# A two-layer cross-attention kernel: the order in the first attention, and a new list of pieces in the second

## The chip, the cores and the metric

The kernel runs on one NeuronCore of a Trainium2 chip. The metric is the device time of one execution in microseconds. A core has five engines that work side by side, each with its own queue in program order: PE (matrix products and transposes, results into PSUM), DVE (vector work), ACT (activations and copies), POOL [...] and SP (which here only issues transfers). They wait for each other through semaphores. [...]

## The reference

All data is float32. `x` and `ctx` have shape (32, 256, 256): batches, tokens, features. The program has two layers.

```python
# L0: 16 heads of 16 features; only batch 0 of the attention is used
q, k, v = heads(x @ Wq.T), heads(ctx @ Wk.T), heads(ctx @ Wv.T)
att = softmax(q @ k.T / 4) @ v
x1 = x + att[0]                       # att of batch 0 is added to every batch

# L1
nX = layernorm(ctx, n1w, n1b)
nF = layernorm(x1, n2w, n2b)
attended = softmax(nF @ nX.T / 16) @ nX          # first attention of L1
h = gelu(attended @ fc1_w.T + fc1_b)             # 4 hidden values
cross = h @ fc2_w.T + fc2_b
nC = layernorm(cross, n3w, n3b)
self_att = softmax(nC @ nC.T / 16) @ nC          # second attention of L1
out = nF + gamma2 * (cross + gamma1 * self_att)
```

Since `cross` is linear in 4 hidden values and a constant, the second attention is done in rows of 5 or 6 values per token rather than 256. Its products have a contraction of at most 32.

## The kernel before

Everything is one function, with a manual schedule: instructions stand on each engine in the order in which the Python code issues them. No scheduler moves them, so a line moved in the code is a line moved in the queues of all the engines that it uses. Batches are handled in fours (`QB = 4`; eight fours, `NQ = 8`).

**L0** (line 680 on). The 16 heads of batch 0 are handled as four fours, `j` = 0 to 3. For each four:
- `head_queries(j)`: the scores by queries, 8 matmuls on PE into four PSUM banks (`four_banks`, which goes round six banks);
- `head_maxima(j, sq, heads)`: DVE takes the row maxima, one instruction of 128 x 512 for each of the four banks;
- `head_less(j)`: PE transposes the maxima (`pm`), and the function that it returns lets DVE add them to the queries (`qmT`);
- `head_keys(j)`: the scores by keys with the maxima in them, then four exponentials on ACT;
- `head_values(j)`: the weighted values and sums on PE (`ph`), and a copy of the column block, `col`, by ACT or DVE;
- `head_turned(j)`: PE transposes the block, and the function that it returns (`weighted`) lets DVE divide and write `att`.

Between these stand `project_values`, the second half of the value projection; `stats(n)`, DVE's statistics of the context of batch n (two instructions of 0.41 us each); `moments_c(q)`, eight short POOL instructions for the layer norm of a four of contexts; `even_normed` (POOL) and `odd_normed` (ACT), which apply it to the even and odd token tile; and `setup_bias`, a small product with DVE's `fc1b_all` behind it, which the first hidden layer needs much later. When `att` is complete, it is added to batch 0 by DVE and to fours of batches by an accumulating DMA that POOL issues (`add_attention`).

Short results of PE go to PSUM tiles of the tag `tp`, of which there are two. A new one takes the bank that was freed first.

**First attention of L1** (`first_step(s)`, one step for each batch, and three more to drain). `scaled_at` says in which step POOL multiplies the skip of batch n by its norm weight (`scale_skip(n)`, one POOL instruction of 128 x 512). Parts of the second attention for early groups are put between these steps.

**Second attention of L1** (`order`, line 1244 on). After the last step the rest is written as a list of pieces, worked off word by word. Groups `g` are fours of batches, pairs `p` two batches. The words: `q7@s1+q6@et` scores by queries of pairs 7 and 6 into the banks `s1` and `et` (an even and an odd pair together use different rows of PE); `max7` DVE's maxima of them; `turn_t`, `turn_u`, `turn_v` transposes and `tT`, `uT`, `vT` the copies of them (ACT, or DVE with `.v`); `k5@s0` scores by keys, `exp5` their exponentials; `sums1` the weighted sums of a group, `col1` their copy, `turn_a1` and `a1` transpose and division; `o1@et` the output product, `add1` DVE's add to the skip and the write of two batches to memory; `scale12` the scaling of a skip. For the last eight batches the hidden layer also stands in the list: `turn_n7`, `n7`, `pre6` (POOL), `gelu6` (ACT), `m3` (POOL, product with a Gram matrix), `vg3` (DVE), `vgv3` (POOL), `var3` (DVE), `r3` (POOL: the power -1/2 and the next Gram product `w_k`), `t_k3` (DVE).

`add p` needs `scale` of both of its batches. A bank (`s0`, `s1` or the two of `et`) is free for the next product once the `max`, `exp` or `add` before has read it. `turn_u6` and `turn_u7` need `t_k3`.

Of the kernel before, what the change touches and what calls it, by code (L numbers as in the profile page):

```python
# [22 lines left out]
QB = 4  # L23
# [4 lines left out]
def tile_xattn_seq(  # L28
# [51 lines left out]
    def bank(tag, name):  # L80
        return ps.tile([P, NC, D], F32, tag=tag, name=name)
# [50 lines left out]
    k6 = const.tile([NK, D], F32)  # L132
# [80 lines left out]
    def moments(st, n, name, eng=None):  # L213

        eng = eng or nc.gpsimd

        def t(what, c=1, bufs=2):
            return small.tile([P, n, c], F32, tag=f"{what}{n}", name=f"{what}_{name}", bufs=bufs)

        sm, df, sq, v4, ve, nm = t("sm", 2), t("df"), t("sq"), t("v4"), t("ve"), t("nmean")  # L220
        rs, nmr = t("rs", 1, 3), t("nmr", 1, 3)
        eng.tensor_sub(df, st[:, :, 1:2], st[:, :, 4:5])
        eng.tensor_add(sm, st[:, :, 1:3], st[:, :, 4:6])
        eng.tensor_mul(sq, df, df)
        eng.tensor_scalar(v4, sm[:, :, 1:2], 4.0 / D, 4 * EPS, ALU.mult, ALU.add)
        eng.tensor_add(ve, v4, sq)
        nc.gpsimd.tensor_tensor(  # L227
            rs.rearrange("p n o -> p (n o)"),
            ve.rearrange("p n o -> p (n o)"),
            neg_half[:, 0:n],  # L230
            ALU.pow,
        )

        def product():
            eng.tensor_scalar(nm, sm[:, :, 0:1], -0.5, 0.0, ALU.mult, ALU.add)
            eng.tensor_mul(nmr, nm, rs)  # L236

        if eng is nc.gpsimd:
            product()
            return rs, nmr  # L240
        return rs, nmr, product
# [19 lines left out]
    def flat(st):  # L261
        return st.rearrange("p b t c -> p (b t) c")

    def moments_c(q):
        rn = moments(flat(st_of[q - 1][:, 0]), TQ, f"c{q}")
        for b in range(QB):
            mc_of[q * QB + b] = *rn, b * NC
# [159 lines left out]
    def project_values(t, copy):  # L427
        pp = bank("tp", f"pp_v{t}")
        for dc in range(NC):
            nc.tensor.matmul(  # L430
                pp[:, t, :],
                c0T[:, dc, t * P : (t + 1) * P],
                wvT[:, dc, :],
                start=(dc == 0),
                stop=(dc == NC - 1),
            )
        copy(v1[:, t, :, 0:DK], pp[:, t, :].rearrange("p (h e) -> p h e", e=DK))

    def pair_products(*pairs):

        for t in range(NC):
            for p, lhs, rhs, dst in pairs:
                for i in range(2):
                    r = SL * (p % 2 * 2 + i)
                    nc.tensor.matmul(  # L445
                        dst[i][:, t, :],
                        lhs[r : r + SL, t * P : (t + 1) * P],
                        rhs[r : r + SL, :],
                        start=True,
                        stop=True,  # L450
                    )
# [4 lines left out]
    def four_banks(name):  # L456

        at = head_banks[0]
        head_banks[0] = (at + QB) % 6
        return [  # L460
            ps0.tile([P, NC, D], F32, tag=f"h{i}", name=f"{name}_{i}")
            if i < QB
            else bank("et", f"{name}_{i}")
            for i in ((at + n) % 6 for n in range(QB))
        ]
# [8 lines left out]
    def head_of(j, i):  # L474
        return 8 * (j // 2) + 2 * i + j % 2

    def head_queries(j):

        sq = four_banks(f"sq{j}")
        qk = qT[:, j, :], kT[:, j, :]  # L480
        pair_products((0, *qk, sq[0:2]), (1, *qk, sq[2:4]))
        return sq

    def head_maxima(j, sq, heads):
        for i in heads:
            nc.vector.tensor_reduce(
                m_all[:, j % 2, :, i, ones_at[j % 2]], sq[i], AX.X, ALU.max, negate=True
            )

    def head_less(j):  # L490
        pm = bank("tp", f"pm_{j}")
        for t in range(NC):
            nc.tensor.transpose(
                pm[:, 0, t * P : (t + 1) * P],
                m_all[:, j % 2, t].rearrange("p b c -> p (b c)"),
                ident,
            )
        return lambda: nc.vector.tensor_add(qmT[:, j % 2, :], pm[:, 0, :], qT[:, j, :])

    def head_keys(j):  # L500

        sk = four_banks(f"sk{j}")
        kq = kT[:, j, :], qmT[:, j % 2, :]
        pair_products((0, *kq, sk[0:2]), (1, *kq, sk[2:4]))
        eT_of[j] = wk.tile([P, QB, NC, D], F32, tag="eTq", name=f"eT_h{j}", bufs=2)
        for i in range(QB):
            nc.scalar.activation(eT_of[j][:, i], sk[i], AF.Exp)
# [4 lines left out]
    def head_values(j, copy=nc.scalar.copy, by_pairs=False):  # L512
        col_of[j] = by_columns(
            tp_bank,
            f"h{j}",
            lambda kt, i: v1[:, kt, head_of(j, i), :],
            eT_of.pop(j),
            copy,
            by_pairs,
        )  # L520

    def head_turned(j):
        pa = tokens_first(tp_bank, col_of.pop(j), f"h{j}")

        def weighted():
            rd = small.tile([P, NC, QB, 1], F32, tag="rdh", name=f"rd_h{j}")
            nc.vector.reciprocal(rd, pa[:, :, :, DK : DK + 1])
            nc.vector.tensor_mul(
                att.rearrange("p t (k i e d) -> p t k i e d", i=QB, e=2, d=DK)[
                    :, :, j // 2, :, j % 2, :  # L530
                ],
                pa[:, :, :, 0:DK],
                rd.to_broadcast([P, NC, QB, DK]),
            )

        return weighted
# [39 lines left out]
    def setup_bias():  # L576
        pb = bank("tp", "p_b1f")
        for dc in range(NC):
            nc.tensor.matmul(
                pb[:, 0, 0:FH], ones, b1f[:, dc, :], start=(dc == 0), stop=(dc == NC - 1)  # L580
            )
        nc.vector.tensor_add(fc1b_all, pb[:, 0, 0:FH], fc1b_bc)
# [78 lines left out]
    on_scalar = nc.scalar.copy  # L661

    by_vector = nc.vector.tensor_copy

    def stats(*ns):
        for n in ns:
            stats_c(n)
# [6 lines left out]
    sq = head_queries(0)  # L674
# [5 lines left out]
    sq = head_queries(1)  # L680
# [9 lines left out]
    head_less(1)()  # L690
    setup_outer()
    stats(3)
    project_values(1, on_scalar)
    moments_c(0)
    even_normed(0, 1, 2, 3)
    sq = head_queries(2)
    stats(4)
    head_maxima(2, sq, (0, 1))
    head_values(0)
    setup_bias()  # L700
    head_maxima(2, sq, (2, 3))
    head_keys(1)
    odd_normed(0, 1)
    weighted = head_turned(0)
    stats(5)
    head_less(2)()
    weighted()
    sq = head_queries(3)
    stats(6)
    head_maxima(3, sq, range(QB))  # L710
    head_values(1)
    odd_normed(2, 3)
    head_keys(2)
    weighted = head_turned(1)
    stats(7)
    moments_c(1)
    even_normed(4, 5)
    head_less(3)()
    weighted()
    head_keys(3)  # L720
    stats(8, 9, 10)
    head_values(2, by_vector)
    stats(11)
    odd_normed(4)
    head_values(3, on_scalar, True)
    c_ends = moments_ahead(2)
    weighted = head_turned(2), head_turned(3)
    for f in weighted:
# [133 lines left out]
    ]  # L862


    scaled_at = [25, 26, 26, 27, 27, 28, 29, 29, 31, 31, 32, 32]

    first_ends = [ends]

# [373 lines left out]


    order = """
    turn_v0 scale12 q7@s1+q6@et t_k2 vT0 scale13 turn_t2 max7 sums1 tT2 scale14 max6
    k5@s0+k4@s1 col1 turn_n7 exp5 scale15 turn_u5 n7 o1@et uT5.v exp4 pre6 turn_t3 add1
    scale16 q11@s1+o0@s0 tT3 gelu6 sums2 max11 scale17 turn_u4 col2 add0 m3 turn_a1 uT4
    k7@s1+q10@et scale18 a1 vg3 turn_a2 q8@s0 max10 exp7 vgv3 scale19 turn_v1 var3
    q9@s1+k6@et a2 vT1 max8 r3 turn_v2 exp6 turn_t5 max9 o2@s0 tT5 vT2 o3@et+k10@s1 add2
    turn_t4 exp10 add3 sums3 k11@s1+o4@s0 tT4.v col3 scale20 t_k3 turn_a3 exp11 add4  # L1250
    turn_u6 scale21 o5@et uT6 a3 scale22 q12@s0+k9@s1 add5 turn_v3 exp9 scale23 max12
    sums5 k8@s1+q13@et col5.v scale24 vT3.v turn_u7 exp8 max13 scale25 o7@s0 uT7 turn_t6
    scale26 add7 q15@et+o6@s1 tT6 turn_a5 scale27 max15 sums4 a5 scale28 q14@s0+k13@et
    col4 add6 turn_a4 exp13 scale29 turn_v5 max14 k12@s1 vT5 a4 scale30 o11@s0+o10@et
    exp12 turn_t7 add11 scale31 sums6 tT7 add10 k15@s1+k14@s0 col6.v turn_v4 exp15
    turn_a6 vT4.v a6 exp14 o8@et+o9@s1 sums7 add9 turn_v6 col7 add8 vT6 turn_a7
    o13@s1+o12@s0 a7 turn_v7 add13 vT7 o14@et add12 o15@s1 add14 add15
    """

    def turn_a(g):  # L1260
# [100 lines left out]
```

## Time and profile before

| | us |
|---|---|
| three runs | 229.31, 230.23, 233.49 (median 230.23) |
| profiled execution | 233.63 |
| its span, first to last instruction | 231.9 |
| PE busy | 214.7 (93%) |
| POOL busy | 174.8 (75%) |
| DVE busy | 169.8 (73%) |
| ACT busy | 146.8 (63%) |
| mean granted PE clock | 0.969 |

The page gives busy time by engine, then the span in 40 slices of 5.8 us (a digit is a share in tenths; PEclk is the granted clock of PE), then the chain of work that ended last, and groups of instructions. A line of the timeline reads: start, duration, engine, line, operation, output<-input, shape, count, and in brackets the idle time before it with what ended it. PEld is the weight load of PE. A busy PE includes the modelled ends of pipelined matmuls.

### The profile page before, as it was taken

Reading aid. Unit: us, or ns where it says so; the run is one execution under the profiler, and the core shown is the slowest. Engines: PE = TensorE matmul, PEld = TensorE weight load, DVE = VectorE, ACT = ScalarE, POOL = GpSimd, SP = SyncE. Lnnn points to the kernel's source line nnn. Section 1 sums busy time; section 2 is a strip of 40 time slices with the busy share of each in tenths; the row PEclk is TensorE's granted clock in tenths of the full one; section 3 lists DMA queues with packets and bytes.
Section 4 is the critical chain, followed back from the end, with each engine's and each line's share of the span. In section 5 each row is a group of like instructions: output and inputs, shape, how many; then the busy total and the mean of one; then the engine's idle time right before and its main releaser. Section 6 shows DMA issues by size and latency. Waiting matters only on the chain.

```text
span 231.9 us, 4950 instructions
## 1 busy us (share of the span) xinstructions
PE 214.7 (93%) x1797; PEld 155.8 (67%) x1797; DVE 169.8 (73%) x409; ACT 146.8 (63%) x299; POOL 174.8 (75%) x276
## 2 busy tenths in 40 slices
PE   7999898898999989999999999989989999999960
PEld 6766556576787768697897887866665666566540
DVE  1797989899988748667686686766384866588791
ACT  2544978698988285966789967456846753444410
POOL 6057598576989999999979999995189999993000
PEclk9999999999999999999999999999999995699996
DMA  6789997999959964180720000000000130444477
GB/s 212 271 310 371 394 383 148 194 256 236 207 104 335 275 117 170 34 151 2 133 51 1 3 0 0 3 4 4 4 0 3 51 133 0 181 184 181 185 281 264
DMA packets 18038, 33.81 MB, mean 146 GB/s; under 512 B 1175, under 2 KB 2142, under 8 KB 18014
## 3 DMA queue, kind: packets, MB, share of 16 engines
q1 hardware_dynamic: 12974, 24.33, 29.3%
q0 software_dynamic: 3696, 7.34, 18.1%
q10 hardware_dynamic: 1344, 1.84, 2.3%
q8 instruction: 14, 0.23, 0.4%
q14 instruction: 10, 0.08, 0.1%
HBM read 17.73 MB, written 8.39 MB: 113 GB/s over the span
## 4 chain that ended last, share of the span: by engine, by line
PE 53%; POOL 23%; DVE 14%; ACT 5%; issue 2%; DVEq 0%; POOLq 0%; ACTq 0%
PE sc L779 13%; POOL x_all L770 5%; PE k L445 4%; PE pt_x L202 4%; PE o L445 3%; PE pt_c L202 3%; POOL cq L307 3%; DVE st L211 3%; PE pt_e L202 3%; PE pu L357 3%; POOL rs_b L227 3%; PE sc L445 2%; POOL rs_x L227 2%; PE ph L357 2%; PE pf L357 2%
## 5 line engine op out<-in xcount | busy, mean ns | idle before, releaser
L779 PE MATMUL sc<-nxT,nfT 128*128 128x256 f32 x256 | 62.4, 386 | 0.7 <-ACT nfT L761 0.7
L779 PEld LDWEIGHTS sc<-nxT,nfT 128*128 128x128 f32 x256 | 45.7, 190 | 12.1 <-issue 5.3
L770 POOL TENSOR_TENSOR x_all<-x_all,w_bc 128x512 f32<-128x512 f32 x32 | 39.8, 1273 | 0.0
L792 ACT ACTIVATE e<-sc,nm 128x256 f32<-128x256 f32 x64 | 26.9, 473 | 19.0 <-DVE nm L789 18.8
L789 DVE TENSOR_REDUCE nm<-sc 128x2 f32<-128x512 f32 x32 | 22.0, 688 | 22.9 <-PE sc L779 11.1
L761 ACT ACTIVATE nfT<-pt_x,bq,wq 128x256 f32<-128x256 f32 x64 | 33.3, 583 | 1.6 <-PE pt_x L202 1.5
L1214 DVE TENSOR_TENSOR x_all<-o,x_all 128x512 f32<-128x512 f32 (+1 forms) x22 | 19.4, 927 | 8.0 <-PE o L445 8.0
L211 DVE BATCH_NORM_STATS2 st<-x_all 128x6 f32<-128x256 f32 x64 | 23.2, 411 | 0.6 <-DMA x_all<-att 0.5
L1209 ACT ACTIVATE eT<-k 128x1024 f32<-128x1024 f32 (+1 forms) x16 | 14.2, 916 | 13.2 <-PE k L445 10.5
L202 PE MATMUL pt_x<-ident,x_all 128*128 128x128 f32 x132 | 20.8, 280 | 1.5 <-POOL x_all L329 1.3
L202 PE MATMUL pt_c<-ident,cq 128*128 128x128 f32 x132 | 19.7, 276 | 1.5 <-ACT nfT L761 1.0
L202 PE MATMUL pt_e<-ident,e 128*128 128x128 f32 x128 | 19.5, 275 | 1.3 <-ACT eTq L801 0.7
L211 DVE BATCH_NORM_STATS2 st<-cq 128x6 f32<-128x256 f32 x56 | 20.6, 412 | 0.0
L307 POOL TENSOR_SCALAR cq<-cq,rs_b,nmr_b 128x256 f32<-128x256 f32 x32 | 19.4, 680 | 0.0
L202 PEld LDWEIGHTS pt_e<-ident,e 128*128 128x128 f32 x128 | 15.4, 141 | 5.0 <-ACT e L792 1.6
L202 PEld LDWEIGHTS pt_x<-ident,x_all 128*128 128x128 f32 x132 | 15.5, 143 | 4.7 <-POOL x_all L329 2.4
L801 ACT COPY eTq<-pt_e 128x512 f32<-128x512 f32 x32 | 18.4, 588 | 0.3 <-PE pt_e L202 0.3
L345 DVE COPY nxT<-pt_c 128x512 f32<-128x512 f32 x23 | 15.6, 677 | 2.3 <-PE pt_c L202 2.3
L202 PEld LDWEIGHTS pt_c<-ident,cq 128*128 128x128 f32 x132 | 15.0, 141 | 3.1 <-ACT nfT L761 1.9
L331 ACT ACTIVATE x_all<-x_all,nmr_b,rs_b 128x256 f32<-128x256 f32 x16 | 9.8, 618 | 10.9 <-POOL nmr_b L236 10.9
L445 PE MATMUL o<-w_out,vt 32*128 32x256 f32 x128 | 15.0, 448 | 0.6 <-ACT vt L1088 0.5
L445 PE MATMUL k<-tt,ut 32*128 32x256 f32 x112 | 15.3, 441 | 0.1
(222 smaller groups left out, 443.8 us busy)
## 6 DMA issues: line engine op xcount, KB each, us to landing
out_dram<-x_all SPq DMA_DIRECT2D x16, 512.0 KB
x_all<-att POOLq DMA_DIRECT2D x7, 1024.0 KB, 9.3
cq<-in_ctx_dram SPq DMA_DIRECT2D x6, 1024.0 KB
x_all<-in_x_dram SPq DMA_DIRECT2D x4, 1024.0 KB
x_all<-in_x_dram SPq DMA_DIRECT2D x1, 2048.0 KB
x_all<-in_x_dram SPq DMA_DIRECT2D x1, 1792.0 KB
cq<-in_ctx_dram ACTq DMA_DIRECT2D x1, 1024.0 KB
cq<-in_ctx_dram SPq DMA_DIRECT2D x1, 768.0 KB
```

The source lines that it names most:

```text
L202: nc.tensor.transpose(pt[:, dc, t * P : (t + 1) * P], src[:, t, dc * P : (dc + 1) * P], ident)
L211: nc.vector.bn_stats(st[:, t, :], src[:, t, :])
L307: nc.gpsimd.tensor_scalar(row, row, rs[:, i + t, :], nmr[:, i + t, :], ALU.mult, ALU.add)
L357: nc.tensor.matmul(pg[SL * b : SL * (b + 1), 0, :], weights(kc, b), moving[:, b, kc, :], start=(kc == 0), stop=(kc == NC - 1),)
L445: nc.tensor.matmul(dst[i][:, t, :], lhs[r : r + SL, t * P : (t + 1) * P], rhs[r : r + SL, :], start=True, stop=True,)
L761: nc.scalar.activation(nfT_of[n][:, dc, :], px[:, dc, :], AF.Identity, bias=bq[:, dc : dc + 1], scale=wq2[:, dc : dc + 1],)
L770: nc.gpsimd.tensor_mul(x_all[:, n], x_all[:, n], w2_bc.unsqueeze(1).to_broadcast([P, NC, D]))
L779: nc.tensor.matmul(sc[:, qt, :], nfT[:, dc, qt * P : (qt + 1) * P], nxT[:, dc, :], start=(dc == 0), stop=(dc == NC - 1),)
L789: nc.vector.tensor_reduce(nm, sc, AX.X, ALU.max, negate=True)
L792: nc.scalar.activation(e[:, qt, :], sc[:, qt, :], AF.Exp, bias=nm[:, qt : qt + 1])
L801: nc.scalar.copy(eT_of[q][:, b], turned(e_of.pop(n), "et", f"e_{n}"))
L1214: nc.vector.tensor_add(xs, po, xs)
```

## The change

In L0, the third four's scores by queries (`head_queries(2)`) go ahead of `project_values(1)`; its maxima are taken in one go instead of two and two; the third four's keys, corrections and statistics are put in another order; `setup_bias` moves to the end; the copy of the third column block goes from DVE to ACT. In the second attention, the list is written anew, and the scalings of batches 10 and 11 move from step 32 of the first attention into the list. All the pieces are the same otherwise.

```diff
     stats(3)
+    sq = head_queries(2)
+    stats(4)
     project_values(1, on_scalar)
     moments_c(0)
     even_normed(0, 1, 2, 3)
-    sq = head_queries(2)
-    stats(4)
-    head_maxima(2, sq, (0, 1))
+    head_maxima(2, sq, range(QB))
+    head_keys(1)
+    head_less(2)()
     head_values(0)
-    setup_bias()
-    head_maxima(2, sq, (2, 3))
-    head_keys(1)
+    stats(5)
+    sq = head_queries(3)
     odd_normed(0, 1)
     weighted = head_turned(0)
-    stats(5)
-    head_less(2)()
-    weighted()
-    sq = head_queries(3)
-    stats(6)
     head_maxima(3, sq, range(QB))
     head_values(1)
     odd_normed(2, 3)
     head_keys(2)
+    head_less(3)()
+    weighted()
+    stats(6)
     weighted = head_turned(1)
+    head_keys(3)
     stats(7)
+    weighted()
     moments_c(1)
     even_normed(4, 5)
-    head_less(3)()
-    weighted()
-    head_keys(3)
+    head_values(2)
     stats(8, 9, 10)
-    head_values(2, by_vector)
+    setup_bias()
+    head_values(3, on_scalar, True)
     stats(11)
     odd_normed(4)
-    head_values(3, on_scalar, True)
     c_ends = moments_ahead(2)
...
-    scaled_at = [25, 26, 26, 27, 27, 28, 29, 29, 31, 31, 32, 32]
+    scaled_at = [25, 26, 26, 27, 27, 28, 29, 29, 31, 31]
...
     order = """
-    turn_v0 scale12 q7@s1+q6@et t_k2 vT0 scale13 turn_t2 max7 sums1 tT2 scale14 max6
-    k5@s0+k4@s1 col1 turn_n7 exp5 scale15 turn_u5 n7 o1@et uT5.v exp4 pre6 turn_t3 add1
-    scale16 q11@s1+o0@s0 tT3 gelu6 sums2 max11 scale17 turn_u4 col2 add0 m3 turn_a1 uT4
-    k7@s1+q10@et scale18 a1 vg3 turn_a2 q8@s0 max10 exp7 vgv3 scale19 turn_v1 var3
-    q9@s1+k6@et a2 vT1 max8 r3 turn_v2 exp6 turn_t5 max9 o2@s0 tT5 vT2 o3@et+k10@s1 add2
-    turn_t4 exp10 add3 sums3 k11@s1+o4@s0 tT4.v col3 scale20 t_k3 turn_a3 exp11 add4
-    turn_u6 scale21 o5@et uT6 a3 scale22 q12@s0+k9@s1 add5 turn_v3 exp9 scale23 max12
-    sums5 k8@s1+q13@et col5.v scale24 vT3.v turn_u7 exp8 max13 scale25 o7@s0 uT7 turn_t6
-    scale26 add7 q15@et+o6@s1 tT6 turn_a5 scale27 max15 sums4 a5 scale28 q14@s0+k13@et
-    col4 add6 turn_a4 exp13 scale29 turn_v5 max14 k12@s1 vT5 a4 scale30 o11@s0+o10@et
-    exp12 turn_t7 add11 scale31 sums6 tT7 add10 k15@s1+k14@s0 col6.v turn_v4 exp15
-    turn_a6 vT4.v a6 exp14 o8@et+o9@s1 sums7 add9 turn_v6 col7 add8 vT6 turn_a7
-    o13@s1+o12@s0 a7 turn_v7 add13 vT7 o14@et add12 o15@s1 add14 add15
+    turn_t2 scale10 q7@s1+q6@et t_k2 tT2 turn_n7 max7 scale11 k5@s0 n7 turn_v0 exp5
+    turn_u4 pre6 vT0.v max6 uT4 scale12 o0@s1+o1@s0 gelu6 turn_t3 add0 sums1 tT3 m3
+    k4@et+q9@s1 col1.v add1 scale13 turn_a1 exp4 turn_u5 max9 scale14 q8@s0 uT5 vg3
+    q11@s1+k6@et a1 vgv3 var3 turn_v1 max8 r3 exp6 sums2 vT1.v k7@s0+q10@et col2 max11
+    turn_a2 exp7 turn_t4 max10 o3@s1 tT4 a2 o2@et+k9@s0 add3 scale15 turn_v2 exp9 sums3
+    vT2.v t_k3 scale16 o5@s0+k8@s1 col3 add2 turn_a3 exp8 scale17 turn_u7 add5 o4@et uT7
+    scale18 a3 q15@s0+q14@s1 add4 scale19 turn_t5 max14 turn_u6 tT5 turn_v3 scale20
+    uT6.v vT3 k10@et+k11@s1 max15 scale21 sums4 exp11 turn_t7 exp10 scale22
+    q12@s1+q13@s0 tT7.v col4.v turn_a4 max12 scale23 sums5 a4 k15@et+o6@s1 col5 scale24
+    max13 turn_a5 exp15 turn_v4 scale25 add6 k14@s0 vT4 a5 scale26 o8@s1+o7@et exp14
+    turn_t6 add8 scale27 sums7 tT6 add7 turn_v5 col7 scale28 o9@s1+k12@s0 vT5 k13@et
+    add9 exp12 scale29 turn_a7 exp13 o10@s0+o11@s1 scale30 a7 sums6 add10 scale31
+    turn_v7 col6 add11 vT7 turn_a6 o15@s0+o14@et a6 turn_v6 add15 vT6 o12@s1 add14
+    o13@s0 add12 add13
     """
```

## The prediction

> **What bounds the kernel now.** I read the page first, then windows over the last 50 us, then the chain of waits, then the timeline of the two places that the change touches: the first attention (L0, up to about 40 us) and the list of pieces (from 176.6 us).
>
> ```profile
> span 231.9 us, 4950 instructions
> PEclk9999999999999999999999999999999995699996
> ...
> 186.00:189.00 3.00, 3.00 (x30) 1.93 (x32) 1.25 (x5) 2.62 (x4) 3.00 (x4) 1.00 0.49 184
> 189.00:192.00 3.00, 2.85 (x17) 1.35 (x14) 2.97 (x7) 0.78 (x2) 2.92 (x5) 0.73 0.02 5
> 192.00:195.00 3.00, 3.00 (x23) 2.43 (x24) 0.85 (x1) 1.24 (x3) 2.84 (x3) 0.50 0.00 0
> 195.00:198.00 3.00, 3.00 (x22) 1.55 (x20) 2.90 (x5) 1.02 (x1) 3.00 (x3) 0.50 0.24 91
> 198.00:201.00 3.00, 3.00 (x29) 1.47 (x21) 0.57 (x1) 0.37 (x1) 3.00 (x3) 0.56 0.69 259
> 201.00:204.00 3.00, 3.00 (x36) 2.19 (x32) 2.62 (x5) 1.58 (x3) 3.00 (x4) 1.00 0.21 80
> ```
>
> The window rows give PE, weight load, DVE, ACT, POOL, then granted clock, DMA share and GB/s. In this execution the clock was 0.50 for some 10 us, in the middle of the list. So the list must be reckoned twice, as it ran and at full clock.
>
> ```profile
> 176.83 7.39 POOL x_all L770 x6
> 184.22 0.27 POOL pre L993
> 184.49 0.07 issue
> 184.56 0.29 POOL pre L995
> 184.85 2.46 POOL x_all L770 x2
> 187.31 0.99 POOL w_m L1010
> 188.30 0.02 issue
> 188.33 0.57 DVE vg L1024
> 188.90 0.61 DVE t_sl L1196
> 189.51 0.04 issue
> 189.55 1.17 PE k L445 x3
> ```
>
> This is the chain of waits: POOL scales six skips before `pre6` and two more before `m3`; DVE waits for `m3` with `vg3`; `max10` stands behind `vg3`; PE waits for `max10` to get the bank for `k6`. From 189.5 to 222 the chain is PE nearly throughout.
>
> ```profile
> 27.75 0.74 DVE L211 BATCH_NORM_STATS2 st<-cq 128x6 f32<-128x256 f32 x2
> 28.51 0.42 DVE L498 TENSOR_TENSOR qmT<-pm,qT 128x256 f32<-128x256 f32 x1
> 28.57 0.21 POOL L222 TENSOR_TENSOR df_c<-st 128x8 f32<-128x8 f32 x1 [2.66 <-DVE st L211]
> 33.26 1.64 POOL L227 TENSOR_TENSOR rs_c<-ve_c,neg_half 128x8 f32<-128x8 f32 x1
> 35.17 1.51 POOL L751 DMA_DIRECT2D x_all<-att  x1 [0.28 <-DVE att L528]
> 37.13 0.72 POOL L227 TENSOR_TENSOR rs_x<-ve_x,neg_half 128x2 f32<-128x2 f32 x1 [0.45 <-DVE ve_x L226]
> ```
>
> In L0, DVE is nearly full from 20.3 to 34.9 us. POOL waits 2.66 us for the last statistics of the second context four (stats 7), and after that has only 0.28 and 0.45 us to spare before it must deliver `rs_x` of the first batch, which is on the chain.
>
> [...] PE idled about 0.15 us between 189 and 190. [...] `max10` waits behind `vg3` though its scores were ready. [...] here two products of opposite parity take 1.08 us (16 matmuls), one alone 1.06 (8). [...]
>
> **Part 1, L0.** The third four's scores go ahead of the second value projection (1.0 us on PE), all four maxima run in one go, `fc1b_all` and its product move to the end, stats 6 and 7 move behind the third and fourth corrections, `odd_normed(4)` moves behind the last column copy, and one column copy (0.41 on DVE) goes to ACT (0.37). Worked out with the durations of before:
> - Scores 2 start at about 18.0 rather than 19.19; DVE is busy with stats 4 to 19.39, so the maxima start at 19.4 (before 20.35) and end at 21.87 (23.27).
> - Keys 1 need the second maximum (20.63): exp from 21.5 (22.97) to 23.56. qmT 2 is at 22.4 (23.92). Scores 3 start at 23.3, maxima 3 at 24.47 (25.36) until 26.94 (27.83). qmT 3 is at 27.5 (28.51). So far about 1 us earlier.
> - It isn't kept. ACT does exp 2 only after two odd norms, at 27.3 (27.56). DVE has waited about 0.5, 1.0 and 0.5 us for PE where it did statistics before; stats 6 and 7 (1.40) now follow qmT 3 and the weighting: 28.26 to 29.66, before 28.49.
> - POOL's moments therefore start at 29.74, not 28.57: 1.17 late. Of this, the 0.28 and 0.45 us of slack take 0.73. Left: 0.45 us on `rs_x` and on all that follows.
> - The last attention column doesn't gain either: its PSUM bank is that of the fc1 bias product, which DVE frees after stats 8, 9, 10 (32.16), so it starts at 32.25 and its copy at 33.4, as before (33.42). Behind it in PE's queue stand the two turns of the columns, for which DVE's weighting waits. The attention is done at about 34.85 both times.
> Part 1: +0.45 us. From 38 to 93 us the chain alternates between DVE and POOL without a gap, then it is PE, so it carries to the end. Bounds: 0 (if POOL's issue of the attention DMA overlaps more) and +0.9 (if it takes its whole 1.51). No landing decides: the DMA issued at 35.17 is first read at 48.41, and it landed in 9.3 us in the median.
>
> **Part 2, the list.** Removed and added work is nil: 15 pairs, 8 singles, 7 sums, 4 turns of u, 22 other turns in both. The two scalings (2 x 1.24 on POOL) leave step 32 but stand first in the new list, so the same 22 run after `w_k2` (176.8). What changes is the order: two instead of six stand before `pre6`, one instead of two before `m3`. Step lengths from the trace, start to next start: pair 1.08, single 1.06, sums 1.00, turn of u 0.62, other turn 0.37 (0.17 before another).
>
> Before, at full clock, from `q9+k6` at 188.70: waits for `max10`, done 190.85; `o2` waits for `max8` until 191.8; `o3+k10` waits for `max9` until 193.0; `turn_t4`, `sums3`, `k11+o4`, to 196.53; `turn_u6` waits for `t_k3` (`w_k` ends 196.13, plus 0.74) until 197.0; `o5`, `q12+k9`, `turn_v3`, `sums5`, `k8+q13`, `turn_u7`, `o7`, `turn_t6`: `q15+o6` at 204.27. It ran at 208.15, so the half clock cost 3.88 us. The last add, 227.0 in the trace, would be at 223.1.
>
> After, from 176.59 in the same way: `pre6` at 179.9 (184.16), `m3` 182.8 (187.27), `r3` from 187.3, `w_k` done 192.35 (196.13), `t_k3` 194.1, and `turn_u7` at 195.06 finds it ready. PE's waits: 0.33 at `o0+o1` (exp 5, `vT0`), 0.16 at `q11+k6`, 0.08 at `o2+k9`, 0.55 at `k10+k11` (`max14`), 0.2 at `o8+o7`, 0.5 at `o12` (`vT6`). Milestones: `sums2` 187.6, `o5+k8` 193.8, `q12+q13` 202.1, `o10+o11` 212.7, `o13` done 219.9. DVE's last add ends at 221.85, against 223.1: -1.27 us. The last scaling ends at 213.6 (210.9 before), ahead of `add15` at 216.9. On SP only the order of the 16 output writes changes. The last four adds are 1.2 us apart in both lists, so the writes behind them (4.9 us from the last add to the end) stay. Bounds: -2.9 (none of PE's new waits) and +0.5 (each taken twice, and 0.2 for wrong bank order).
>
> **Sum.** The profiled execution took 233.63 us (span 231.9 and 1.7 around it). At full clock: 233.63 - 3.88 = 229.75, between the runs 229.31 and 230.23 (median 230.23). Change: +0.45 - 1.27 = -0.8. Predicted: 228.9 us, 0.6% under the median.
>
> **Rivals.**
> - A, forecast, 0.57: as worked out, 228.9, own range 227.6 to 230.4.
> - B, both parts better, 0.16: L0 keeps half of its early maxima (-0.5) and the list has none of its waits (-2.9): 229.75 - 3.4 = 226.4. For: qmT 3 is 1 us early. Against: POOL's start after stats 7.
> - C, slower, 0.19: the half clock falls into most executions. Place: the list, where PE works with 32 rows and waits in short stretches; price: 3.9 us less about 0.4 that other engines then hide, 228.9 + 3.5 = 232.4. [...] most likely at `k10+k11`. For: the profiled execution shows it. Against: my list has shorter waits, and two of three runs of before have no room for it.
> - D, slower, 0.08: in L0 the late moments also delay the even norms and with them the first context turns, +2 us, and the list gives nothing: 231.8. Against: the turns of the second context four come after 35 us.
> That the list doesn't do what it says is no rival: counts and parities are equal.
>
> **How the numbers follow.** The likeliest case gives 228.9. Leaving out no more than 0.2: 226.3 to 232.6, which holds A, most of B and most of C. Two per cent is about what a measurement of this kernel can tell from no change: below 225.6 only the outer part of B (0.11 with room for what I did not see), above 234.8 the outer parts of C and D (0.07), within 0.82.
>
> **What would show it.** Right: maxima 2 in one row from 19.4; POOL's `df_c` at 29.7 and `rs_x` 0.45 late; first scores (L778) near 40.7; `m3` near 182.8 plus that delay; `t_k3` no longer ahead of a PE wait; last add near 222.3. Wrong: `rs_x` early or on time; a PE wait of over 1 us in the list; the last scaling later than `o15`; a clock of 0.50 in the list.

## The result, and the profile after

The changed kernel takes 228.26 us in the median (227.76 to 230.69), the kernel before 229.66 beside it (228.43 to 233.57). The ratio is 0.9968, with a 95% interval of 0.9951 to 0.9985: 0.3% faster, a small gain, but clear of the noise. The forecast was 228.9 us. Executions of over 233 us (15 of the 95 of the kernel before that were timed in all, and one of E4 below) are left out of every ratio here.

The profiled execution of after took 228.26 us, its span 226.5. That is 5.4 us less than in the profile of before, but most of this is the half clock in that one execution of before. First the page of after, its PEclk row, and its windows over the list (columns as before).

```profile
span 226.5 us, 4957 instructions
PEclk9999999999999999999999999999999999999995
...
186.00:189.00 3.00, 3.00 (x42) 1.74 (x38) 2.85 (x7) 1.57 (x4) 2.22 (x4) 1.00 0.46 175
189.00:192.00 3.00, 3.00 (x42) 2.12 (x38) 2.92 (x6) 1.67 (x4) 2.84 (x3) 1.00 0.02 5
192.00:195.00 3.00, 3.00 (x48) 1.80 (x44) 2.95 (x6) 1.40 (x2) 3.00 (x3) 1.00 0.27 102
195.00:198.00 3.00, 3.00 (x38) 2.04 (x30) 2.79 (x6) 1.50 (x2) 3.00 (x4) 1.00 0.70 262
198.00:201.00 3.00, 2.92 (x32) 2.00 (x32) 3.00 (x4) 0.86 (x3) 3.00 (x3) 1.00 0.89 336
```

The fives and sixes of before in PEclk are gone, and the clock is 1.00 in every window of the list, from 174 to 219 us. PE has next to no gap there.

The timeline of POOL and DVE in L0, for the lines that were shown of before:

```profile
27.27 0.42 DVE L498 TENSOR_TENSOR qmT<-pm,qT 128x256 f32<-128x256 f32 x1 [0.65 <-ACT cq L322]
28.05 1.40 DVE L211 BATCH_NORM_STATS2 st<-cq 128x6 f32<-128x256 f32 x4
29.52 0.21 POOL L222 TENSOR_TENSOR df_c<-st 128x8 f32<-128x8 f32 x1 [3.92 <-DVE st L211]
34.05 1.64 POOL L227 TENSOR_TENSOR rs_c<-ve_c,neg_half 128x8 f32<-128x8 f32 x1
35.63 1.46 POOL L750 DMA_DIRECT2D x_all<-att  x1
36.97 0.89 POOL L227 TENSOR_TENSOR rs_x<-ve_x,neg_half 128x2 f32<-128x2 f32 x1
37.89 0.41 DVE L236 TENSOR_TENSOR nmr_x<-nmean_x,rs_x 128x2 f32<-128x2 f32 x1 [0.34 <-POOL rs_x L227]
38.34 0.94 DVE L329 TENSOR_SCALAR x_all<-x_all,rs_x,nmr_x 128x256 f32<-128x256 f32 x1
38.50 2.30 POOL L316 TENSOR_SCALAR cq<-cq,rs_c,nmr_c 128x256 f32<-128x256 f32 x2
```

POOL now waits 3.92 us for stats 6 and 7, and the two pauses of 0.28 and 0.45 us that it had before the attention's DMA and before `rs_x` are gone: it runs without a gap from 34.05. The chain of waits goes the same way (start, duration, engine and output, line):

```profile
28.13 1.32 DVE st L211 x4
30.73 1.66 POOL rs_c L227
...
34.05 1.64 POOL rs_c L227
35.68 1.41 POOL x_all L750
37.10 0.77 POOL rs_x L227
37.89 0.42 DVE nmr_x L236
38.34 0.94 DVE x_all L329
```

So POOL carries the chain from the statistics to the first layer norm. In before the same stretch of the chain ran over PE's products and DVE's add of the attention:

```profile
28.99 1.15 PE sk L445 x16
30.14 3.25 PE ph L357 x32
34.89 0.70 DVE x_all L828
35.61 0.76 DVE st L211 x2
```

POOL in the list of after:

```profile
180.43 0.30 POOL L992 TENSOR_TENSOR pre<-n_all,rd_f 128x64 f32<-128x64 f32 x1 [0.55 <-DVE rd_f L986]
183.32 1.03 POOL L1009 TENSOR_TENSOR w_m<-v_sl,gram_m 128x400 f32<-128x400 f32 x1 [0.99 <-ACT v_sl L995]
188.21 2.92 POOL L1047 TENSOR_TENSOR r<-ve,neg_half 128x16 f32<-128x16 f32 x1
191.64 1.34 POOL L1009 TENSOR_TENSOR w_k<-u_sl,gram_k 128x576 f32<-128x576 f32 x1
```

`pre6` and `m3` no longer stand behind six and two scalings. They wait for other engines, as the brackets say, and come about 4 us sooner (184.16 and 187.27 before).

**Three lengths.** The traced executions differ by up to 0.9 us in when L0 begins, ahead of every edited instruction. So I measure between marks: A from the scores by keys of four 0 (the `sk` row of the timeline that starts at 15.5 to 16.5 us) to the first scores of L1 (L778); C from there to the start of the maximum of the last batch (`nm`, near 172); B from that to the end of the last add. In before A is 40.29 - 16.10 = 24.19; the other rows are made in the same way.

| kernel | A | C | B | ratio to before, 95% interval |
|---|---|---|---|---|
| before (half clock in the list) | 24.19 | 131.54 | 55.16 | 1 |
| after | 24.84 | 131.78 | 49.16 | 0.9968, 0.9951 to 0.9985 |
| E1 new L0 alone | 25.87 | 131.59 | 50.73 | 1.0055, 1.0035 to 1.0074 |
| E2 new list alone | 24.19 | 131.50 | 49.16 | 0.9932, 0.9907 to 0.9957 |
| E3 before, POOL's scalings moved | 24.19 | 131.51 | 49.03 | 0.9949, 0.9927 to 0.9972 |
| E4 after, four scalings early | 24.83 | 131.64 | 51.35 | 1.0081, 1.0052 to 1.0109 |
| E5 after, stats 6 and 7 early | 23.65 | 131.37 | 49.16 | 0.9914, 0.9891 to 0.9936 |
| E6 after, bias product late | 24.82 | 131.73 | 49.23 | 0.9986, 0.9968 to 1.0004 |
| E7 E5 and E6 | 23.66 | 131.50 | 49.16 | 0.9919, 0.9898 to 0.9940 |
| E8 E7, odd scaling of group 4 early | 23.66 | 131.54 | 49.16 | 0.9933, 0.9907 to 0.9958 |
| E9 E2, moments late | 24.52 | 131.61 | 49.23 | 0.9957, 0.9939 to 0.9975 |
| E10 E5's L0, E3's list | 23.65 | 131.34 | 49.02 | 0.9924, 0.9905 to 0.9944 |

C is nearly constant (131.34 to 131.78): what L0 loses or gains is carried through 130 us with little change.

### The profile page after: what moved, and what is told of

The parts are those of the page before. It is cut to its first block, busy times and chain, and to the rows that moved or that the text cites. A ratio compares the mean times of both kernels' runs of the same rounds, so it can differ in the third digit from the quotient of the medians.

```text
span 226.5 us, 4957 instructions
## 1 busy us (share of the span) xinstructions
PE 207.1 (91%) x1797; PEld 152.5 (67%) x1797; DVE 170.1 (75%) x405; ACT 146.6 (65%) x302; POOL 175.4 (77%) x276
## 4 chain that ended last, share of the span: by engine, by line
PE 53%; POOL 18%; DVE 11%; ACT 5%; issue 2%; DVEq 1%; POOLq 0%; ACTq 0%
PE sc L778 15%; PE o L445 4%; PE k L445 4%; PE pu L357 4%; PE pt_e L202 3%; POOL cq L307 3%; PE pt_x L202 3%; PE pt_c L202 3%; DVE st L211 3%; PE pv L357 3%; POOL rs_b L227 3%; PE sc L445 2%; PE q L445 2%; POOL rs_c L227 2%; POOL rs_x L227 2%
## 5 line engine op out<-in xcount | busy, mean ns | idle before, releaser
L778 PE MATMUL sc<-nxT,nfT 128*128 128x256 f32 x256 | 62.4, 386 | 0.9 <-ACT nfT L760 0.9
L778 PEld LDWEIGHTS sc<-nxT,nfT 128*128 128x128 f32 x256 | 45.7, 190 | 12.3 <-issue 5.3
L1213 DVE TENSOR_TENSOR x_all<-o,x_all 128x1024 f32<-128x1024 f32 (+1 forms) x20 | 19.3, 1005 | 2.9 <-PE o L445 2.4
L1208 ACT ACTIVATE eT<-k 128x512 f32<-128x512 f32 (+1 forms) x19 | 14.3, 799 | 9.1 <-PE k L445 7.8
L307 POOL TENSOR_SCALAR cq<-cq,rs_b,nmr_b 128x256 f32<-128x256 f32 x32 | 19.4, 680 | 0.0
L202 PEld LDWEIGHTS pt_x<-ident,x_all 128*128 128x128 f32 x132 | 15.5, 143 | 5.4 <-POOL x_all L329 2.6
L445 PE MATMUL o<-w_out,vt 32*128 32x256 f32 x128 | 13.3, 400 | 0.6 <-ACT vt L1087 0.5
L445 PE MATMUL k<-tt,ut 32*128 32x256 f32 x112 | 13.6, 397 | 0.0
```

What stands on the lines that cost most here:

```text
L202: nc.tensor.transpose(pt[:, dc, t * P : (t + 1) * P], src[:, t, dc * P : (dc + 1) * P], ident)
L307: nc.gpsimd.tensor_scalar(row, row, rs[:, i + t, :], nmr[:, i + t, :], ALU.mult, ALU.add)
L445: nc.tensor.matmul(dst[i][:, t, :], lhs[r : r + SL, t * P : (t + 1) * P], rhs[r : r + SL, :], start=True, stop=True,)
L778: nc.tensor.matmul(sc[:, qt, :], nfT[:, dc, qt * P : (qt + 1) * P], nxT[:, dc, :], start=(dc == 0), stop=(dc == NC - 1),)
L1213: nc.vector.tensor_add(xs, po, xs)
```

## The experiments

**E1: the new L0 alone.** L0 as in after, the list and `scaled_at` as in before. Against after:

```diff
-    scaled_at = [25, 26, 26, 27, 27, 28, 29, 29, 31, 31]
+    scaled_at = [25, 26, 26, 27, 27, 28, 29, 29, 31, 31, 32, 32]
...
-    turn_t2 scale10 q7@s1+q6@et t_k2 tT2 turn_n7 max7 scale11 k5@s0 n7 turn_v0 exp5
+    turn_v0 scale12 q7@s1+q6@et t_k2 vT0 scale13 turn_t2 max7 sums1 tT2 scale14 max6
...
```

> The first attention in the new order, the old list of pieces. Theory (the two parts have opposite signs): POOL's moments of the second context four start about 1.2 us late behind DVE's statistics, and some 0.45 to 0.65 us of it reaches rs_x of the first batch and stays to the end: 0.2 to 0.3% slower than before, ratio 1.002 to 1.003. Rival (the first attention gains by its earlier maxima, the list does little): ratio 0.997 or lower.

Measured: 230.22 us, ratio 1.0055. The sign holds, the loss is about twice the expected one (0.0055 of 229.2 is 1.3 us). The profiled execution (231.24 us) is slower than the median, and its trace shows why. Windows of E1:

```profile
31.00:32.00 1.00, 0.41 (x4) 0.32 (x3) 1.00 (x4) 1.00 (x4) 0.87 (x2) 1.00 1.07 393
32.00:33.00 1.00, 0.34 (x8) 0.33 (x12) 1.00 (x5) 0.27 (x2) 1.00 (x2) 1.00 1.03 371
...
34.00:35.00 1.00, 0.82 (x6) 0.71 (x5) 0.65 (x3) 1.00 (x3) 1.00 (x3) 0.55 1.01 371
35.00:36.00 1.00, 1.00 (x7) 1.00 (x6) 0.91 (x3) 0.36 (x2) 1.00 (x1) 0.50 0.34 121
36.00:37.00 1.00, 1.00 (x6) 1.00 (x6) 0.97 (x3) 0.74 (x3) 1.00 (x2) 0.50 0.10 37
37.00:38.00 1.00, 1.00 (x9) 1.00 (x8) 0.83 (x6) 0.52 (x1) 0.71 (x2) 0.74 0.00 0
```

PE is 1.25 us idle from 31.4 on, waiting for `fc1b_all`, and from 34.1 to 37.5 it runs at half clock (0.50). A is 25.87 in this execution, 1.03 more than in after: a copy of DVE waits 0.99 us for PE's transposes there, and the first layer norm stands behind it. This doesn't explain the median. Four of the 22 executions have a mean clock of 0.982 to 0.984, all others 0.988 or more, and without these four the median is still 230.11. The profile of after has the same wait, also 1.25 us, and keeps 1.00 in its windows from 30 to 42 us; its A of 24.84 is L0's price at full clock, +0.65. B is 50.73 in E1: the old list at full clock (1.00 in the windows from 186 to 210 us). So the half clock cost the profiled execution of before 55.16 - 50.73 = 4.4 us.

**E2: the new list alone.** The reverse: L0 as in before, the list and `scaled_at` as in after. Against after:

```diff
-    sq = head_queries(2)
-    stats(4)
     project_values(1, on_scalar)
     moments_c(0)
     even_normed(0, 1, 2, 3)
+    sq = head_queries(2)
+    stats(4)
+    head_maxima(2, sq, (0, 1))
...
```

> The first attention in the old order, the new list with its two scalings. Theory: the list alone gives about 1.3 us, ratio 0.994 to 0.995, and with the loss of the first attention this makes the 0.997 of the whole change. No half clock inside the list in the profile. Rival (the list only ends the half clock and does nothing otherwise): ratio 0.999 to 1.001.

Measured: 227.73 us, 0.9932, a little under the expected range, which lies in the interval; the rival's range is excluded, and the list runs at full clock (nines in PEclk up to its last slice). B is 49.16: 1.57 us less than the old list at full clock. The list's gain is real and L0 takes part of it back.

**E3: only POOL's order in the old list.** Eight words moved, no other piece:

```diff
-    turn_v0 scale12 q7@s1+q6@et t_k2 vT0 scale13 turn_t2 max7 sums1 tT2 scale14 max6
+    turn_v0 q7@s1+q6@et t_k2 vT0 turn_t2 max7 sums1 tT2 max6
...
-    q9@s1+k6@et a2 vT1 max8 r3 turn_v2 exp6 turn_t5 max9 ...
+    q9@s1+k6@et a2 vT1 max8 r3 scale12 scale13 scale14 scale15 scale16 scale17 scale18 scale19 turn_v2 ...
```

(and `scale15` to `scale19` taken out of their places between)

> The old list and the old first attention, with one thing changed: the scalings 12 to 19, which stood ahead of and between pre6, m3, vgv3 and r3 on POOL, stand behind r3. Theory (the gain of the list comes from POOL: t_k3 and max10 no longer come late): w_k of r3 is done some 3 us earlier, PE's waits at q9+k6 (0.6 us) and turn_u6 (0.3 us) go, and 0.5 to 0.9 us is gained, ratio 0.996 to 0.998. Rival (the gain is the order of PE's products and of the last adds, not POOL's): ratio 0.999 to 1.001 though w_k is early.

Measured: 227.98 us, 0.9949: more than the theory's 0.996 to 0.998, of which a part lies in the interval. The rival's range is excluded. The timeline of POOL in E3:

```profile
181.83 0.30 POOL L993 TENSOR_TENSOR pre<-n_all,rd_f 128x64 f32<-128x64 f32 x1 [2.24 <-DVE rd_f L987]
185.15 1.03 POOL L1010 TENSOR_TENSOR w_m<-v_sl,gram_m 128x400 f32<-128x400 f32 x1 [2.65 <-ACT v_sl L996]
```

POOL now idles ahead of both and limits nothing; B is 49.03, as short as the rewritten list's 49.16, and 1.70 us under E1's 50.73. PE has the same products in the same order in E1 and E3, so their starts can be compared, counted from `nm`. E3 is level up to `q9`, 1.2 us ahead behind `q9+k6`, 1.6 behind `o3+k10` and 1.7 behind `turn_u6`. So the wait at `q9+k6`, where PE needs `max10`, which stands behind `m3`, was worth about twice the 0.6 us expected.

**E4: the new list with four scalings ahead of `pre6`.** Against after:

```diff
-    turn_u4 pre6 vT0.v max6 uT4 scale12 o0@s1+o1@s0 gelu6 ...
+    turn_u4 scale12 scale13 scale14 scale15 pre6 vT0.v max6 uT4 o0@s1+o1@s0 gelu6 ...
```

(and `scale13` to `scale15` taken out of their places behind)

> The whole change, with one thing altered: the scalings 12 to 15 stand ahead of pre6 again, as they did before the change, so that m3, vgv3, r3 and t_k3 come about 5 us less one scaling, some 3.7 us, later. Theory: turn_u7, which comes at about 195.5 us, then waits for t_k3 for 2 to 4 us; ratio to before 1.003 to 1.013. Rival (POOL's order is hidden by PE either way): ratio 0.997 as the whole change.

Measured: 230.78 us, 1.0081, 1.1% above after and in the expected range, but not by the expected wait: `t_k3` ends at 196.62, ahead of `turn_u7` at 197.78. POOL runs `scale10` to `scale15` in one go. ACT stands idle for 2.50 us ahead of `gelu6`, which needs `pre6`; the copies `tT3` and `uT5` stand behind it in ACT's queue, and PE waits for both. POOL's timeline, then PE's, of E4:

```profile
177.45 7.42 POOL L769 TENSOR_TENSOR x_all<-x_all,w_bc 128x512 f32<-128x512 f32 x6
184.82 0.31 POOL L992 TENSOR_TENSOR pre<-n_all,rd_f 128x64 f32<-128x64 f32 x1
...
186.10 0.44 PE L1116 MATMUL pt_a<-ident,col_u 128*128 128x128 f32 x2 [1.13 <-ACT tt L1087]
188.98 0.48 PE L445 MATMUL q<-ut 32*128 32x256 f32 x2 [0.94 <-ACT ut L1077]
```

1.13 + 0.94 = 2.07 us of waits; B grew by 2.19. In this execution the clock stayed at 1.00 even behind them (windows from 186 to 195 us); three of the other eleven have a mean clock of 0.977 to 0.985.

**E5: the statistics of groups 6 and 7 earlier in the new L0.** They now stand in DVE's idle time ahead of the maxima and of `qmT` of four 3:

```diff
     weighted = head_turned(0)
+    stats(6)
     head_maxima(3, sq, range(QB))
...
     head_keys(2)
+    stats(7)
     head_less(3)()
     weighted()
-    stats(6)
     weighted = head_turned(1)
     head_keys(3)
-    stats(7)
     weighted()
     moments_c(1)
```

> The changed kernel with one edit: the statistics of groups 6 and 7 stand ahead of the maxima of four 3 and ahead of the subtraction of four 3, where VectorE is idle 0.92 and 0.65 us in the changed kernel's profile. Ratios are to the kernel before; the changed kernel stands at 0.9968. Theory (the moments of groups 4 to 7, started on POOL at 29.5 instead of 28.6 us, are what the new order costs): POOL's df_c starts near 27.5, rs_x ends about 0.9 us earlier against the first projection, and the kernel stands near 0.993 to 0.995. Rival 1 (the cost is the 1.25 us for which the fourth's value product waits for the bias product's reader, which stays or grows here): same as the changed kernel, 0.996 to 0.998. Rival 2 (VectorE has no room there after all: the two statistics delay the maxima of four 3): slower than the changed kernel, 0.998 to 1.001.

Measured: 227.12 us, 0.9914, better than the theory's 0.993 to 0.995. Its interval lies wholly under that of after. POOL and DVE of E5:

```profile
27.07 0.21 POOL L222 TENSOR_TENSOR df_c<-st 128x8 f32<-128x8 f32 x1 [1.77 <-DVE st L211]
36.01 0.71 POOL L227 TENSOR_TENSOR rs_x<-ve_x,neg_half 128x2 f32<-128x2 f32 x1 [0.44 <-DVE ve_x L226]
36.95 0.66 DVE L329 TENSOR_SCALAR x_all<-x_all,rs_x,nmr_x 128x256 f32<-128x256 f32 x1
```

The moments start 2.2 us sooner against the mark, POOL has its 0.44 us to spare again, and A falls from 24.84 to 23.65, 0.54 under before. Here about half of the 1 us by which the scores come earlier is kept.

**E6: the bias product late.** Against after:

```diff
     stats(8, 9, 10)
-    setup_bias()
     head_values(3, on_scalar, True)
...
     turned_4()
+    setup_bias()
     ends(nc.vector)
```

> The changed kernel with one edit: the first layer's bias product (p_b1f, fc1b_all) is made behind the last transposes of context instead of between the value products of fours 2 and 3, so that four 3's product needs no bank that a late VectorE instruction frees. Theory (POOL's late moments are the cost, the wait of TensorE lies beside them): the wait of 1.25 us is gone from the trace, the first attention ends some 0.9 us earlier, but rs_x and the first scores come as late as before, and the ratio stays at 0.996 to 0.998. Rival (the wait is the cost): 0.993 to 0.995. Third: the wait is what lets TensorE fall to half its clock behind it, as in the profile of the kernel with the new first attention alone; then the profile shows 1.00 from 33 to 40 us and the ratio gains up to 0.002 over the theory's.

Measured: 228.83 us, 0.9986, just above the theory's range; the rival's range lies below the interval, and the third's gain isn't seen. PE's wait of 1.25 us is gone, the profile shows 1.00 in its windows from 30 to 40 us, but A is 24.82, as in after. The attention's end moved less than expected: the copy of the last column (33.20 in E6, 33.26 in after) is 0.66 us earlier against the mark, but DVE's first add of `att` (35.05 and 34.73) only 0.28, since its weighting stands behind its own moments of the third four of contexts. And POOL's moments, late as before, hide even that.

**E7: both edits.**

> The changed kernel with both edits: the statistics of groups 6 and 7 earlier and the bias product later. Theory: POOL's moments and the attention's end both move ahead by about 0.9 us, so that the first scores stand 0.9 to 1.6 us earlier than in the changed kernel, counted from the first projection; ratio to the kernel before 0.989 to 0.993. If the two edits only shift the same wait onto something else (the transposes of context on TensorE, the copies on ScalarE): no better than the better one of the two alone, 0.993 to 0.996.

Measured: 227.10 us, 0.9919, A 23.66. The ratio lies in the theory's range, but E5 alone gives the same: the two edits don't add up. With early moments PE's wait for the bias in E5 is only 0.35 us; nothing is left to win there.

**E8: E7 with the odd scaling of group 4 earlier.** Against E7:

```diff
+    stats(11)
+    odd_normed(4)
     head_values(3, on_scalar, True)
-    stats(11)
-    odd_normed(4)
```

> As the kernel with both edits, and with the odd scaling of group 4 ahead of the value product of four 3 in ScalarE's order. ScalarE is idle there, waiting for four 3's exponentials' product, while the scaling waits for POOL's moments, so it either fills that idle time (0.2 to 0.5 us earlier than with both, ratio 0.987 to 0.992) or, if the moments are late, it holds the copy of the product behind it (0.5 us later than with both, 0.991 to 0.996).

Measured: 227.19 us, 0.9933, A 23.66: neither the expected gain nor the expected loss. The scaling runs earlier (31.62 us, 33.49 in E7 with a start 0.52 later), but A doesn't change: ACT isn't the limit there.

**E9: the old L0 with late moments.** Nothing else of the new L0 is in it. Against E2:

```diff
     sq = head_queries(3)
-    stats(6)
...
     weighted = head_turned(1)
+    head_less(3)()
+    stats(6)
     stats(7)
     moments_c(1)
     even_normed(4, 5)
-    head_less(3)()
```

> The kernel with the new list alone (ratio 0.9932 to the kernel before), with one edit in its old first attention: the statistics of groups 6 and 7, the moments of groups 4 to 7 and the even scalings 4 and 5 stand behind the subtraction of four 3, as in the changed kernel; nothing else of the new first attention is in it. POOL's df_c starts near 30.1 us on the scale of the kernel before (28.57 there). Theory (late moments cost, whatever the order of scores and projection): first scores 0.6 to 1.1 us later against the second queries' product than in the kernel with the new list alone, ratio 0.996 to 0.999. Rival (POOL had slack for it and the loss lies in another part of the new order): 0.992 to 0.995, first scores less than 0.2 us later.

Measured: 228.00 us, 0.9957, between the two ranges (E2 0.9932, intervals overlap), so the times decide nothing. In the trace the lateness alone does cost: A is 24.52, 0.33 more than in E2. `df_c` is 1.33 us late against the mark (30.09 - 16.29 = 13.80, before 28.57 - 16.10 = 12.47). `rs_x` ends at 38.49 - 16.29 = 22.20, before at 37.85 - 16.10 = 21.75: 0.45 late. So the path absorbs 0.88 of the 1.33; my 0.73 was near, and 0.6 to 1.1 in the expectation was too much.

**E10: E5's L0 with E3's list.** The diffs of E5 and E3 together.

> The new first attention with the statistics of groups 6 and 7 earlier, and the list of the kernel before with only POOL's eight scalings 12 to 19 moved behind r3. Theory (what the new list gives is POOL's early m3 and nothing else): from the last maximum of the first layer's last step to the last sum it takes 49.0 us as in the kernel with that move alone (49.2 with the new list), and the ratio is that of the kernel with the statistics earlier, 0.990 to 0.993. Rival (the new order of pieces has a gain of its own of about 0.3 us): 0.993 to 0.995.

Measured: 227.06 us, 0.9924, A 23.65 and B 49.02: the lengths of E5 and E3, side by side. The interval of the ratio (0.9905 to 0.9944) doesn't exclude the rival's range; the length B does. The rewritten order of pieces adds nothing to moving POOL's eight scalings. E5, E7 and E10, 227.1 us each, beat both kernels and can't be told apart.

## Why the prediction was right, point by point

**The forecast case came in.** Predicted were 228.9 us and "+0.45 - 1.27" from two causes. (The "0.6%" is against 230.23, a median of three; against the prediction's own start at full clock, 229.75, it is 0.4%.) The signs of both are shown by E1 (slower) and E2 (faster). The sum of the profiles closes: half clock -4.43, A +0.65, C +0.24, list -1.57, earlier start -0.29, together -5.40, and the spans differ by 5.4. The two parts of the change, with C, come to 0.65 + 0.24 - 1.57 = -0.7 us; the ratio 0.9968 is -0.7 of 229.7. That this comes so near the forecast -0.8 is in part luck: L0 lost 0.20 more than forecast, C, which had no term, 0.24, and the list gained 0.30 more.

**Part 1's course was right up to POOL.** With the start of after moved by 0.29 us onto the scale of before: maxima 2 in one row from 19.3 (predicted 19.4), `qmT` 3 at 27.56 (27.5), stats 6 and 7 ending at 29.74 (29.66), `df_c` at 29.81 (29.74), the fc1 bias freed at 32.2 (32.16), four 3's product at 32.34 (32.25).

**Part 1's size was not: the term "Left: 0.45 us" is +0.65.** `rs_x` itself is only 0.30 late (37.86 - 15.81 = 22.05 against 21.75). The other 0.35 stands behind it, and I had priced it at nothing. DVE makes the layer norm while POOL issues the second attention DMA and then scales contexts. This is so in before too, but in after `nmr_x` takes 0.41 and L329 0.94, where before had 0.16 and 0.66, as these lines of before show:

```profile
37.88 0.16 DVE L236 TENSOR_TENSOR nmr_x<-nmean_x,rs_x 128x2 f32<-128x2 f32 x1 [0.17 <-POOL rs_x L227]
38.08 0.66 DVE L329 TENSOR_SCALAR x_all<-x_all,rs_x,nmr_x 128x256 f32<-128x256 f32 x1
38.66 1.64 POOL L316 TENSOR_SCALAR cq<-cq,rs_c,nmr_c 128x256 f32<-128x256 f32 x2
```

From the end of `rs_x` to PE's first transpose behind the layer norm it is 1.13 us in before (37.85 to 38.98) and 1.48 in after (37.86 to 39.34), which is the 0.35. POOL pays too: 2.30 for its two scalings instead of 1.64. So both are longer where L329 and L316 start 0.16 us apart (after) rather than 0.58 (before); why was not shown. E9 has 0.45 us between them, L329 at 0.69, and loses 0.33 with `rs_x` 0.45 late, without such an extra. By time, L0's cost is 0.8 us (after over E2, 0.0036 of 229.4) to 1.3 (E1). The first agrees with A and C of after, 0.65 + 0.24; the 0.4 more in E1 is not resolved.

**Part 2: the course was right, the cause narrower than the working.** With 0.59 us taken off, by which its list starts later (POOL's first scaling at 177.38 for 176.79), after has `pre6` at 179.84 (predicted 179.9), `m3` 182.73 (182.8), `sums2` 187.59 (187.6), `w_k` done at 192.4 (192.35), `turn_u7` 194.95 (195.06), the last scaling ending at 213.34 (213.6). `t_k3` is no longer ahead of a PE wait:

```profile
193.63 0.74 DVE L1054 TENSOR_REDUCE t_sl<-w_k 128x96 f32<-128x576 f32 x1
195.54 0.38 PE L1062 MATMUL pt_u<-ident,u_sl 128*128 128x128 f32 x2
```

Of PE's waits that I listed, one is seen with its size: 0.52 at `o12` (0.5). From `o5+k8` on the list runs ahead of my milestones: 193.6 for 193.8, `q12+q13` 201.55 for 202.1, `o10+o11` 211.85 for 212.7, last add 221.0 for 221.85. My two list lengths were both too long, the new one by 0.85 and the old one at full clock by 0.54 (223.1, E1 222.56 on that scale). Since both errors have one sign, the difference, -1.57 for -1.27, is off by only 0.3. For the same reason the half clock's price of 3.88 us was too small; it is 4.43. E3 and E10 show what the working did not say: the 15 pairs in a new order give nothing, POOL's order gives all.

**The rivals.** A is the forecast. B's list without waits (-2.9) isn't reached by any kernel; 49.02 is the shortest. C stays out: the clock is 1.00 in the list, and of 22 executions of after none is near 233.5 us, while before has five (E1, with the old list, has none either). The wait that it named, at `k10+k11`, shows only as a row of 1.46 us where a full pair's is 1.15 (`q15+q14`). The length of PE's waits, on which its "Against" rests, does not decide it alone, though: after waits 1.25 us in L0 and stays at full clock (see the last section). And the half clock did find a place in L0: in E1, and two of the 22 executions of after have a mean clock of 0.979, where they lost it is not traced. D's mechanism is right in direction, with 0.65 us for its 2.

**The check list.** "`rs_x` 0.45 late" was 0.30, first scores "near 40.7" are 40.65, or 40.94 on the scale of before, which is 0.2 late and the mis-sized term again. The last add, "near 222.3", is at 221.59, or 221.88 on that scale. None of the four signs that it was wrong appeared.

## What to carry to other kernels

When a step is pulled forward on one engine, look at what its old neighbours on the next engine did in that time: here DVE's statistics were filling the wait for PE, and moving them behind it made another engine, POOL, the one that comes last; putting two calls back (E5) turned +0.65 us into -0.54. When a rewritten schedule gains, move only the instructions of the one engine that the chain names: eight words gave the whole of the list's gain. And before a before-profile is compared with an after-profile, take the clock out of it: 4.4 of the 5.4 us between these two were the half clock of one execution.

## What was not expected of the hardware

**The half clock did not go with the length of a wait.** E1 and after have the same PE wait in L0, 1.25 us. In E1 the granted clock was 0.50 from 34.1 to 37.5 us, behind it; in after it was 1.00 in every window from 30 to 42 us. In before's list it was 0.50 from 190.4 to 200.6 us, with PE idle for about 0.15 us ahead of it (189.40 to 189.55). E4's two waits of 1.13 and 0.94 us in the list were followed by 1.00 up to 195 us.

Nor do the executions without a trace go by this wait alone. After, E1, E4 and E6 have two to four executions each with a mean clock of 0.985 or less; the traces of after, E1 and E4 have the wait of 1.25 us, but in E6's it is gone, and two of its 14 executions are at 0.978 and 0.980. None of the 42 executions of E2, E3, E5, E7, E8 and E10, and none of E9's ten, is below 0.986. What brings the half clock was not shown, and no kernel was built to test it.

**A DMA issue on POOL went with a longer DVE instruction beside it.** L329 of the first batch, the same DVE instruction in each kernel, takes 0.41 us in E1, 0.66 to 0.69 in before, E2, E3, E5, E9 and E10, and 0.94 in after and E4. POOL's second DMA issue in before (its L329, at 38.08, is shown above), then both in E1:

```profile
37.81 1.31 POOL L751 DMA_DIRECT2D x_all<-att  x1
...
38.67 1.31 POOL L750 DMA_DIRECT2D x_all<-att  x1
40.39 0.41 DVE L329 TENSOR_SCALAR x_all<-x_all,rs_x,nmr_x 128x256 f32<-128x256 f32 x1
```

In before, E2, E3, E5 and E10 L329 starts 0.26 or 0.27 us behind the start of POOL's second DMA issue and ends 0.92 or 0.93 us behind it; in E1 it starts 1.72 us behind, when the issue is over. In after and E4 it starts 0.69 and 0.68 us behind the issue, and the scalings on POOL start 0.16 us behind L329. That a part of before's 0.66 is a wait for POOL's issue, and that there is more of it in after and E4, is my reading of these rows and was not shown: in E1 L329 runs beside the scalings too (2.21 us from 39.52). On this chain, which alternates between the two engines, the shift of one against the other had a price of its own, the 0.35 us of after. A kernel with this DMA issued behind the layer norm was not tried.
